# A fifth stored form set for a Strassen-like graph product, with six of a set's additions done by accumulating DMAs

## The chip, the cores and the metric

The kernel runs on one core of a Trainium2 chip. The metric is the device time of one execution in microseconds (us), as the median of several runs.

The engines are named as in the profile. PE is TensorE and does the matrix products, PEld is its weight load, DVE is VectorE, ACT is ScalarE, POOL is GpSimd and SP is SyncE. SP only issues DMAs here. SP's and POOL's queues are worked off in order.

## The reference, cut to what matters

Four graph layers run one after the other on `x` (8 batches, 2048 nodes, 64 features). Each adds its result to `x` and normalises over the features. All of them multiply by the same 2048x2048 matrix `adj`.

```
layer 0:  As = [I, A, 2*A@A - I];  out = sum_k (As[k] @ x) @ w[node, k] + b[node]
layer 1:  z = relu((A @ x) @ W0);  out = relu((A @ z) @ W1)
layer 2:  out = x @ W_self + (A @ x) @ W_neighbor + bias
layer 3:  x1 = A @ x;  x2 = 2*A @ x1 - x;  out = cat(x, x1, x2, x1, x2) @ W + bias
each:     x = layernorm(x + out)
```

Layers 0, 1 and 3 need two products with `A`, layer 2 needs one. There are seven products of a 2048x2048 by a 2048x512 matrix, all in float32.

## The kernel before

**Products.** Product 1 (the slices, up to line 1433) also writes sums of blocks of `A` to DRAM (`comb`, seven quarter matrices of four blocks plus four sums each). Products 2 to 7 are the six calls of `product` at lines 1547, 1589, 1620, 1621, 1628 and 1629. Each is one level of Strassen-Winograd on quarters: seven blocks A11, S1, A12, S2, S4, S3, A22 in this order (lines 756 to 835), where S1 to S4 are sums and differences of quarters. Each block multiplies a 1024x1024 quarter by a 1024x256 one. S3 is the difference A11 - A21, the "third difference of quarters".

**Two ways to do a block.** `inner` (line 514) does a second Strassen-Winograd level: seven products of 512x512 blocks, each from 1 MB loaded from the input or from `comb`. Its four sums of `x` (`less`, line 532) are on DVE. `fast_inner` (line 380) does a scheme with 26 products of 256x256 blocks in 13 pairs. Its sums of `x` are twelve POOL additions (lines 404 to 416), its joins are on DVE, and the matrices that it multiplies by, the 26 *forms* of a quarter, are read from DRAM (`formed`). Products 5 and 7 write their result with nodes on partitions (`onto_slot=1`). Their instructions are 128 columns wide, so those of L558 and L437 take the place of L565 and L443 in products 2, 3, 4 and 6.

**Forms.** `make_forms` (line 262) loads the four 1 MB blocks of a quarter, stores four raw parts of them as forms (`RAW`) and works through `SUMS`: 28 additions per set, ten of them on POOL (`POOLED`) and 18 on DVE, 22 of whose results are forms and six only intermediate. Each result tile is one of nine buffers `t` (`TB`). SP stores each form (256 KB) after the next addition has been written down. The next set's loads begin when the present set is nearly through (`k > SPENT`). Forms exist for four quarters (`FORMED`: S1, A12, S2, S4). S1's are made in product 2, the others at the start of product 3. Products 3 to 7 use all four. S3, A11 and A22 always go through `inner`.

**Order of work.** Results of a block go to the "pump", a queue of feature jobs (`hand_over`, line 682). In product 2 the pump is held. Four `feature0` jobs run after S2 (line 804), and the remaining twelve at the start of product 3 (line 713). A `feature0` job is eight steps of twelve PE instructions (L1519), followed by work on DVE (L1529), on ACT (L1533) and on POOL (L1539, L1542). The ACT results `s` have two buffers. `Pump.run` hands out steps of side jobs, `make_forms` first and `prepare_sums` (four DVE sums for the next `inner`, line 698) after it, at a rate per step: 1.28 after S2, 1.08 at the start of product 3. A step in which a postponed normalisation does something gives one side step less. Side steps that are left at the end are written down behind the last job.

**Order on an engine.** What passes through `tc.keep_in_program_order` stays where the program has it. Other instructions may be moved by the scheduler. `inner`'s `less` is pinned like this while the pump is held (line 530), so in all of product 2 after S1.

**After S3.** `last` (line 815) adds v and u, in products 5 and 7 also adds the result into its place in `xy`, and hands the job over. With `inner` it runs block by block as S3 proceeds; with `fast_inner` `last_all` does all four blocks behind S3's last join.

Of the kernel before, what the change touches and what calls it, by code (L numbers as in the profile page):

```python
# [9 lines left out]
F32 = mybir.dt.float32  # L10
AF = mybir.ActivationFunctionType
ALU = mybir.AluOpType
# [4 lines left out]
P = 128  # L17
# [4 lines left out]

A11, A12, A22, S1, S2, S3, S4 = range(7)
A21 = 7
FORMED = (S1, A12, S2, S4)

# [8 lines left out]
ROWS = ((0, 0), (1, 0), (0, 1), (1, 1))  # L37
RAW = {11: (2, 2), 14: (1, 1), 19: (0, 2), 23: (1, 0)}
SUMS = (
    (16, (0, 1), (0, 3), 1), (5, (2, 0), (2, 3), 1), ("d", (2, 1), (2, 2), 1), ("c", (0, 0), (0, 2), 1),  # L40
    (6, 16, (1, 3), 0), (18, 6, "d", 1), (21, (1, 1), "d", 1), (4, 21, (1, 2), 1),
    (1, (1, 3), (2, 3), 1), (2, 1, (2, 0), 1), (15, 2, "c", -1), (0, "c", (1, 0), 0),
    (20, (1, 2), 0, -1), (10, (3, 1), (3, 2), 1), ("f", 10, (3, 3), 1), (17, "f", 1, -1),
    (7, (0, 1), 10, -1), ("b", (0, 0), (1, 0), 1), (12, (0, 3), (1, 3), 1), (24, (3, 0), (3, 2), 1),
    (3, (2, 0), 24, -1), ("a", (1, 1), (2, 1), 1), (8, (3, 0), (2, 0), -1), (22, (3, 1), (0, 1), -1),
    (9, 7, "b", -1), ("e", 24, (3, 3), 1), (13, "e", 12, -1), (25, 3, "a", -1),
)
HALF = {13: 0, 22: 0, 8: 1, 17: 1}
POOLED = {5, 18, 4, 15, 20, 17, 12, 22, 9, 25}
SPENT = 24  # L50


def unit(i, j):
# [89 lines left out]
def kernel(  # L143
# [28 lines left out]
    RING = 4  # L172
    TB = 9
    LANDING = 4
    BLK = TG * GW

    big = ctx.enter_context(tc.tile_pool(name="big", bufs=1))
# [59 lines left out]
    pieces = []  # L237
    p_mm = p_y = None

    def load(q, s, forms=False):  # L240
        nonlocal loads
        loads += 1
        turn = loads % (RING + 3)
        pool = ring2 if ring2 is not None and turn >= RING else ring
        a = pool.tile([P, TG, TG, P], F32, tag="a", name="a")
        flat = a.rearrange("p n m c -> p (n m c)")
        if forms:
            size = min(4, len(SLOT) - 4 * s) * GW
            fetched = nc.sync.dma_start(flat[:, :size], formed[q][s][:, :size])
        elif q in (A11, A12, A22) and s < 4:  # L250
            i, j = {A11: (0, 0), A12: (0, 2), A22: (2, 2)}[q]
            fetched = nc.sync.dma_start(a, blocks[i + s // 2, j + s % 2])
        else:
            fetched = nc.sync.dma_start(flat, comb[q][s])
        if ring2 is not None and loads <= RING + 3:

            tc.keep_in_program_order(fetched)
        if pieces and loads > RING and loads % 3 == 0:
            tc.keep_in_program_order(pieces.pop(0)())
        return a  # L260

    def make_forms(*qs):
# [1 line left out]

        pin = tc.keep_in_program_order

        def store(q, n, f):
            k = SLOT[n]
            dst = formed[q][k // 4][:, ts(k % 4, GW)]
            nc.sync.dma_start(dst.rearrange("p (n m c) -> p n m c", n=2, m=2), f)  # L270

        coming = [load(qs[0], s) for s in range(4)]
        for _ in range(LANDING):
            yield
        for i, q in enumerate(qs):
            tiles, coming, made, done = coming, [], {}, []

            def raw(i, k):
                a, b = ROWS[i]
                return tiles[2 * a + k // 2][:, 2 * b : 2 * b + 2, 2 * (k % 2) : 2 * (k % 2) + 2, :]  # L280

            def source(f):
                return raw(*f) if isinstance(f, tuple) else made[f]

            for n, ik in RAW.items():
                store(q, n, raw(*ik))
            for k, (n, a, b, sign) in enumerate(SUMS):
                f = sums.tile([P, 2, 2, P], F32, tag="t", name="form", bufs=TB)
                if sign == 0:
                    pin(nc.vector.scalar_tensor_tensor(f, source(a), -1.0, source(b), ALU.mult, ALU.subtract))  # L290
                else:
                    eng = nc.gpsimd if n in POOLED else nc.vector
                    pin(eng.tensor_tensor(f, source(a), source(b), ALU.add if sign > 0 else ALU.subtract))
                made[n] = f
                if not isinstance(n, str):
                    done.append((q, n, f))
                yield
                while len(done) > 1:
                    store(*done.pop(0))
                if k > SPENT and len(coming) < 2 and i + 1 < len(qs):  # L300
                    coming.append(load(qs[i + 1], len(coming)))
            for job in done:
                store(*job)
            while len(coming) < 4 and i + 1 < len(qs):
                coming.append(load(qs[i + 1], len(coming)))

    def product(src, feature, between=None, rate=1, own=None, pin=False, runs=None, onto_slot=None, ends=False, fast=(), forms={}):

# [401 lines left out]
            return [make_forms(*forms[q]), prepare_sums(b)] if q in forms else []  # L710

        if waits:
            pump.run(None, side(A11, b11), 1.08)
            pump.hold = False
        pump.pass_mark()

# [84 lines left out]
            fast_inner(S2, t2, InTile(u), None, join_all)  # L801
        else:
            inner(S2, t2, *onto(u, u, then=join))
        pump.run(runs.get(S2, 0), side(S2, b22), 1.28)
        if S4 not in fast:
            inner(S4, b22, *onto(c, c, (0, 1)), ready=ready)
        elif give:
# [153 lines left out]
    if True:  # L961
# [490 lines left out]
        if True:  # L1452
# [91 lines left out]


            RUNS = {A12: 1, S2: NP}
            product(1, then(feature0, 0, gap=4), lambda: pump.add(sum_wn()), rate=4, runs=RUNS, forms={S2: (S1,)})


    late = p_z = None  # L1550
# [35 lines left out]
        nc.vector.scalar_tensor_tensor(part(g, p, 0), z, 0.0, part(g, p, 0), ALU.max, ALU.add)  # L1586
        yield

    product(0, feature1a, to_late, pin=True, fast=FORMED, forms={A11: (A12, S2, S4)})
    def both_terms(src, w, b):  # L1590

        def own(g, p):
# [86 lines left out]
```

## Time and profile before

| what | value |
|---|---|
| median of three runs | 1648.97 us (1647.35 to 1649.34) |
| the profiled execution: its own time | 1647.88 us |
| the profiled execution: its span | 1646.0 us |
| PE busy in the span | 1623.3 us, 99% |
| PEld, DVE, POOL, ACT busy | 1154.6, 1122.0, 574.5, 308.7 us |
| PE clock granted, mean | 0.998 |
| DMA | 429.47 MB, 261 GB/s |

The profiled execution's time has 1.9 us around its span and is 1.1 us below the median. A matrix product in float32 shows as two PE instructions, which overlap: the mean duration of one (say 592 ns) is longer than the distance to the next (429 ns). What a block costs is read from the chain of waits, where rows give a start, a length and a count. Stages in us from the span's start: product 1 to 209, product 2's blocks to 306 and from 389 to 464, `feature0` from 306 to 389 and from 464 to 711, products 3 to 7 from 715 on.

### The profile page before, as it was taken

The page shows a single profiled execution, that of the slowest core. Times are in us where ns is not written, and L with a number is a line of the kernel's source. Part 1 is how long each engine was busy: PE and PEld are TensorE (multiplying, and loading weights), DVE is VectorE, ACT ScalarE, POOL GpSimd, SP SyncE. Part 2 cuts the span into 40 slices and gives each one's busy share as a digit, 9 for nine tenths or more (in the row PEclk, how much of TensorE's full clock was granted, in tenths as well). Part 3 has the DMA queues.
Part 4 walks back from the last instruction along what each step waited for, and adds up shares of the span by engine and source line. Part 5 has one row for each costly group of instructions (what it writes and reads, how often), then busy time and mean ns, then how long its engine had stood idle before and what let it go on. Part 6 is the DMA issues. An engine that isn't in the chain of part 4 may idle for free.

```text
span 1646.0 us, 23252 instructions
## 1 busy us (share of the span) xinstructions
PE 1623.3 (99%) x8886; PEld 1154.6 (70%) x8886; DVE 1122.0 (68%) x1889; ACT 308.7 (19%) x870; POOL 574.5 (35%) x582
## 2 busy tenths in 40 slices
PE   9999999999999999999999999999999999999998
PEld 5998944444444444438865787589999788669998
DVE  5996885686458878846753477974688556644687
ACT  0210100143024444421111111221111112100111
POOL 1121100284037778764502350034512441025510
PEclk9999999999999999999999999999999999999999
DMA  8999999746853645278777776566888866677885
GB/s 315 358 389 370 334 342 326 250 141 237 307 178 123 203 141 187 101 310 312 277 287 262 288 280 253 208 227 234 295 293 301 292 234 213 237 255 282 310 307 175
DMA packets 101390, 429.47 MB, mean 261 GB/s; under 512 B 10752, under 2 KB 31616, under 8 KB 61856
## 3 DMA queue, kind: packets, MB, share of 16 engines
q1 hardware_dynamic: 87616, 380.34, 64.8%
q0 software_dynamic: 12016, 46.27, 7.5%
q8 instruction: 71, 1.16, 0.3%
q10 hardware_dynamic: 1648, 1.38, 0.3%
q14 instruction: 39, 0.32, 0.1%
HBM read 346.16 MB, written 81.79 MB: 260 GB/s over the span
## 4 chain that ended last, share of the span: by engine, by line
PE 94%; DVE 3%; DMA 1%; issue 1%; POOL 0%; ACT 0%; ACTq 0%; SPq 0%; DVEq 0%; POOLq 0%
PE y L1519 19%; PE mm L443 15%; PE mm L437 10%; PE mmb L565 10%; PE mmc L565 7%; PE mma L565 7%; PE ps_n L1301 6%; PE mmb L558 4%; PE ps_i L1215 3%; PE z L1573 3%; PE mmc L558 2%; PE mma L558 2%; PE z L1602 2%; PE ps_n L1255 1%; PE pt L1564 1%
## 5 line engine op out<-in xcount | busy, mean ns | idle before, releaser
L1539 POOL TENSOR_TENSOR s<-s 128x512 f32<-128x512 f32 (+2 forms) x192 | 166.2, 865 | 254.3 <-ACT s L1533 244.1
L1529 DVE SCALAR_TENSOR_TENSOR xy<-y,e_sb,xy 128x128 f32<-128x128 f32 x512 | 179.4, 350 | 65.3 <-PE y L1519 49.4
L1533 ACT ACTIVATE s<-y,e_sb 128x128 f32<-128x128 f32 x512 | 139.3, 383 | 196.2 <-PE y L1519 178.3
L565 PE MATMUL mmb<-a,t 128*128 128x512 f32 x360 | 161.9, 592 | 0.0
L443 PE MATMUL mm<-a,f 128*128 128x256 f32 x576 | 135.1, 380 | 1.1 <-POOL f L389 1.0
L1519 PE MATMUL y<-wn,xT 64*128 64x512 f32 x512 | 131.4, 590 | 0.0
L1519 PE MATMUL y<-wn,C 64*128 64x512 f32 x512 | 131.2, 589 | 0.0
L1519 PE MATMUL y<-wn,tT 64*128 64x512 f32 x512 | 131.1, 589 | 0.0
L389 POOL TENSOR_TENSOR f<-T 128x512 f32<-128x512 f32 x20 | 26.5, 1340 | 276.7 <-PE mmb L565 124.7
L565 PEld LDWEIGHTS mmb<-a,t 128*128 128x128 f32 x360 | 67.3, 190 | 79.4 <-issue 78.7
L443 PEld LDWEIGHTS mm<-a,f 128*128 128x128 f32 x576 | 108.7, 190 | 17.7 <-POOL f L389 1.9
L437 PE MATMUL mm<-f,a 128*128 128x128 f32 x768 | 92.4, 275 | 0.0
L1519 PEld LDWEIGHTS y<-wn,xT 64*128 64x128 f32 x512 | 49.5, 187 | 60.9 <-issue 57.3
L1519 PEld LDWEIGHTS y<-wn,tT 64*128 64x128 f32 x512 | 49.6, 187 | 60.2 <-issue 59.7
L1519 PEld LDWEIGHTS y<-wn,C 64*128 64x128 f32 x512 | 49.5, 187 | 60.4 <-issue 60.4
L437 PEld LDWEIGHTS mm<-f,a 128*128 128x128 f32 x768 | 89.0, 192 | 0.1
L476 DVE TENSOR_TENSOR p<-p,mm 128x512 f32<-128x512 f32 x60 | 41.0, 684 | 61.3 <-PE mm L443 41.7
L319 DVE TENSOR_TENSOR u<-mmb,p 128x512 f32<-128x512 f32 x44 | 30.2, 686 | 67.5 <-PE mmb L565 58.1
L466 DVE TENSOR_TENSOR C<-C,mm 128x512 f32<-128x512 f32 x80 | 54.2, 684 | 29.3 <-PE mm L443 22.3
L565 PE MATMUL mma<-a,T 128*128 128x512 f32 x160 | 72.1, 593 | 0.0
L1023 POOL DMA_DIRECT2D comb<-si x29 | 22.0, 758 | 137.8 <-DVE si L1014 137.8
L558 PE MATMUL mmb<-t,a 128*128 128x128 f32 x576 | 67.3, 275 | 0.0
(243 smaller groups left out, 3024.7 us busy)
## 6 DMA issues: line engine op xcount, KB each, us to landing
a<-comb SPq DMA_DIRECT2D x127, 1024.0 KB, 5.0
a<-form SPq DMA_DIRECT2D x120, 1024.0 KB, 4.8
a<-in_blocks SPq DMA_DIRECT2D x43, 1024.0 KB, 4.9
comb<-si POOLq DMA_DIRECT2D x29, 1024.0 KB, 10.6
form<-form SPq DMA_DIRECT2D x88, 256.0 KB, 2.8
a<-in_slices SPq DMA_DIRECT2D x15, 1024.0 KB, 10.9
comb<-so POOLq DMA_DIRECT2D x15, 1024.0 KB, 12.8
a<-form SPq DMA_DIRECT2D x20, 512.0 KB, 4.8
```

The costliest lines, as they stand in the source:

```text
L437: nc.tensor.matmul(ps[:, ts(2 * h + j, P)], a[:, j, m, :], x[:, m, :], start=(start and h == j == m == 0), stop=(m == 1), skip_group_check ...
L443: nc.tensor.matmul(ps[:, ts(h, GW // 2)], x[:, m, :], a[:, :, m, :], start=(start and h == m == 0), stop=(m == 1), skip_group_check=True,)
L466: nc.vector.tensor_tensor(out, out, view(v), op)
L558: nc.tensor.matmul(to, a[:, k, m, :], xb[:, m, :], start=(start and opens and m == 0), stop=(m == TG - 1), skip_group_check=True,)
L565: nc.tensor.matmul(ps, xb[:, m, :], a[:, :, m, :], start=(start and m == 0), stop=(m == TG - 1), skip_group_check=True,)
L1215: nc.tensor.matmul(ps, x[:, m // 2, m % 2], s[n](m), start=(start and m == 0), stop=(m == TG - 1), skip_group_check=True,)
L1301: nc.tensor.matmul(ps[:, ts(p, GW // 2)], b(k, p), a(k // TG, k % TG), start=(start and p == k == 0), stop=(k == NT // 2 - 1), skip_group_ ...
L1519: mm = nc.tensor.matmul(y[:, b, :], terms[n][half, ts(k, P)], wn[half, n, h * DH : (h + 1) * DH, :], start=(n == 0), stop=(n == 2),)
L1529: tc.keep_in_program_order(nc.vector.scalar_tensor_tensor(acc, y[:, :, ts(d, F)], e, acc, ALU.mult, ALU.add))
L1533: nc.scalar.activation(s[:, d], y[:, :, ts(d, F)], AF.Copy, scale=e)
L1539: nc.gpsimd.tensor_tensor(s[:, :n], s[:, :n], s[:, n : 2 * n], ALU.add)
L1573: nc.tensor.matmul(z[:, k, :], aT[:, ts(k, P)], wd[:, w, :], start=(n == 0), stop=(n == len(terms) - 1),)
```

## The change

S3 becomes a fifth formed quarter. Its set is made after S2 in product 2, in the place of S1's, whose set moves to the start of product 3 as the first of four. S3 goes through `fast_inner` in products 2 to 7.

Six of the 28 additions of a set (forms 5, 4, 15, 18, 9, 25; sign 2) are not done on an engine any more. SP stores the first operand in the form's place in DRAM, and some steps later POOL issues a DMA that adds the second operand onto that place. A set has 22 engine additions left, seven of them on POOL and 15 on DVE. The order of `SUMS` is another one. Loads of the next set start at `k >= 12`. When several sets are made, each set's last two blocks land in buffers `T` and not in the ring. The rates become 1.1 and 1.16.

```
-FORMED = (S1, A12, S2, S4)
+FORMED = (S1, A12, S2, S4, S3)
 SUMS = (
+    (5, (2, 0), (2, 3), 2), ("c", (0, 0), (0, 2), 0), (16, (0, 1), (0, 3), 1), ("d", (2, 1), (2, 2), 1),
+    (0, "c", (1, 0), -1), (21, (1, 1), "d", 1), (4, 21, (1, 2), 2), (1, (1, 3), (2, 3), 1),
+    (2, 1, (2, 0), 1), (15, "c", 2, 2), (6, 16, (1, 3), 0), (18, "d", 6, 2), (20, (1, 2), 0, -1),
+    (10, (3, 1), (3, 2), 1), ("f", 10, (3, 3), 1), (17, "f", 1, -1), (7, (0, 1), 10, -1),
+    ("b", (0, 0), (1, 0), 0), (9, 7, "b", 2), (24, (3, 0), (3, 2), 1), (3, (2, 0), 24, -1),
+    ("a", (1, 1), (2, 1), 0), (25, 3, "a", 2), (8, (3, 0), (2, 0), -1), (22, (3, 1), (0, 1), -1),
+    (12, (0, 3), (1, 3), 1), ("e", 24, (3, 3), 1), (13, "e", 12, -1),
 )
-POOLED = {5, 18, 4, 15, 20, 17, 12, 22, 9, 25}
-SPENT = 24
+POOLED = {20, 17, 22, 12, 8, 13, 1}
+AHEAD_OF_NEXT = (12, 12, 12, 27)
...
+    JOIN = 2
...
+        def fetch(q, s):
+            return load(q, s, home=None if len(qs) == 1 or s < 2 else sums.tile(
+                [P, NT // 2, 4 * F], F32, tag="T", name="T", bufs=3
+            ).rearrange("p t c -> p (t c)").rearrange("p (n m c) -> p n m c", n=TG, m=TG))
...
+            def settle(step):
+                while done and done[0][0] < step:
+                    _, n, f = done.pop(0)
+                    nc.sync.dma_start(slot(q, n), f)
+                while joins and joins[0][0] + JOIN < step:
+                    _, n, f = joins.pop(0)
+                    pin(nc.gpsimd.dma_start(slot(q, n), f, accum_op=ALU.add))
...
             for k, (n, a, b, sign) in enumerate(SUMS):
+                if sign == 2:
+                    done.append((step, n, source(a)))
+                    joins.append((step, n, source(b)))
+                    continue
...
                 yield
-                while len(done) > 1:
-                    store(*done.pop(0))
-                if k > SPENT and len(coming) < 2 and i + 1 < len(qs):
-                    coming.append(load(qs[i + 1], len(coming)))
-            for job in done:
-                store(*job)
-            while len(coming) < 4 and i + 1 < len(qs):
-                coming.append(load(qs[i + 1], len(coming)))
+                settle(step)
+                while i + 1 < len(qs) and len(coming) < 4 and k >= AHEAD_OF_NEXT[len(coming)]:
+                    coming.append(fetch(qs[i + 1], len(coming)))
+            settle(step + JOIN + 2)
...
-            pump.run(None, side(A11, b11), 1.08)
+            pump.run(None, side(A11, b11), 1.16)
...
-        pump.run(runs.get(S2, 0), side(S2, b22), 1.28)
+        pump.run(runs.get(S2, 0), side(S2, b22), 1.1)
...
-            product(1, then(feature0, 0, gap=4), lambda: pump.add(sum_wn()), rate=4, runs=RUNS, forms={S2: (S1,)})
+            product(1, then(feature0, 0, gap=4), lambda: pump.add(sum_wn()), rate=4, runs=RUNS, forms={S2: (S3,)}, fast=(S3,))
...
-    product(0, feature1a, to_late, pin=True, fast=FORMED, forms={A11: (A12, S2, S4)})
+    product(0, feature1a, to_late, pin=True, fast=FORMED, forms={A11: (S1, A12, S2, S4)})
```

## The prediction

> **What bounds the kernel now.** I read the page first: shares, then the chain that ended last, then the same chain in order of time, then the waits of PE, then the queues around the one place where PE stands still.
>
> ```profile
> span 1646.0 us, 23252 instructions
> ...
> PE 1623.3 (99%) x8886; PEld 1154.6 (70%) x8886; DVE 1122.0 (68%) x1889; ACT 308.7 (19%) x870; POOL 574.5 (35%) x582
> ...
> PE 94%; DVE 3%; DMA 1%; issue 1%; POOL 0%; ACT 0%; ACTq 0%; SPq 0%; DVEq 0%; POOLq 0%
> ```
>
> PE is busy 99% of the span, at full clock, and it is the chain. A change gains by what it takes from PE's work or from the 23 us in which PE stands, and loses by what it makes PE wait for.
>
> The chain in order of time gives a block its price: 216 instructions of plain `fast_inner`; an `inner` with 128 columns, whose seven products take 3.57 each; a plain `inner` from 1268.31 to 1292.34, where the next block begins; and three `fast_inner` with 128 columns in one piece (624).
>
> ```profile
> 918.75 46.62 PE mm L443 x216
> ...
> 1218.28 3.57 PE mma L558 x32
> ...
> 1268.31 3.44 PE mma L565 x8
> ...
> 1292.34 24.17 PE mm L443 x112
> ...
> 1494.34 69.69 PE mm L437 x624
> ```
>
> The longest wait of PE is at product 3's first load (waits: us, times, longest), which stands behind the forms' stores in SP's queue (start, length, count) and delays PE's first product:
>
> ```profile
> PE mma L565 <- DMA a<-in_blocks: 3.6, 1, 3.6
> ```
>
> ```profile
> 674.79 33.40 SPq L270 DMA_DIRECT2D form<-form  x11
> 708.25 0.42 SPq L252 DMA_DIRECT2D a<-in_blocks  x1
> ```
>
> ```profile
> 715.03 5.29 PE L565 MATMUL mma<-a,xy 128*128 128x512 f32 x8 [3.61 <-DMA a<-in_blocks]
> ```
>
> **Term 1, S3 by 26 products: -9.9 us.** Plain `inner`: 1292.34 - 1268.31 = 24.03. Plain `fast_inner` has 104 instructions: 46.62 / 216 x 104 = 22.45. It saves 1.58, in products 2, 3, 4 and 6: 6.3. With 128 columns `inner` takes 7 x 3.574 = 25.02 and `fast_inner` 208 x 69.69 / 624 = 23.23, so 1.79, in products 5 and 7: 3.6. All of it is on PE's path. Loads fall too (6.5 MB for 7 MB a block). Nothing of PE's work is added: the forms are made on DVE, POOL and DMA.
>
> **Term 2, the start of product 3: -3.8 (0 to -5.5).** SP's last form store waits for POOL's last form (706.58 to 707.84), the loads stand behind it, and the first lands at 715.0, 6.7 after its issue. PE was through at 711.4. It stands 3.6, then runs its first product in 5.29 instead of 3.44, so 5.5 in all. Counting the pump's steps by the rates (96 job steps, 12 of them with a normalisation): before, 1.08 x 96 - 12 = 91 side steps are handed out of the 4 + 84 + 4 wanted, and the last form goes out at job step 91. After, 1.16 x 96 - 12 = 99 for 4 + 88 + 4, and the last form goes out at step 88. Three job steps of 12 x 0.215 = 2.6 us are 7.7 us: the loads go out near 700.6, and land before 711.4. Two ring buffers are free for them, since a set's last two blocks land elsewhere. What is late next: the loads that use the freed space of `feature0` go out after POOL's last addition (718.38). With the 5.0 of such a load they land at 723.4, and the fourth product wants one at 711.4 + 3 x 3.43 = 721.7. That gives 1.7 back.
>
> **Term 3, S3 to A22 in product 2: +2.3 (0 to +3.7).** There `less` is pinned behind all earlier DVE work. Before, DVE needs only two additions and two sums until PE's second product:
>
> ```profile
> 440.02 0.69 DVE L319 TENSOR_TENSOR C<-mmc,C 128x512 f32<-128x512 f32 x1 [2.02 <-PE mmc L565]
> 440.75 0.69 DVE L319 TENSOR_TENSOR C<-C 128x512 f32<-128x512 f32 x1
> 441.36 0.68 DVE L534 TENSOR_TENSOR t<-T 128x512 f32<-128x512 f32 x1
> 442.07 0.69 DVE L534 TENSOR_TENSOR t<-T,t 128x512 f32<-128x512 f32 x1
> ```
>
> ```profile
> 443.25 3.60 PE L565 MATMUL mmb<-a,t 128*128 128x512 f32 x8
> ```
>
> After, behind S3's last product stand the last joins (0.69 + 0.75), four additions of `last_all` (2.9) and two sums (1.4): 5.7. A22's first product covers 3.43. Its third and fourth sum, if they came first, would add 1.4. If the sums were moved ahead it costs nothing.
>
> **Term 4, the same place in the others: +2.4 (0 to +8).** There the sums are not pinned, and the trace shows A22's already during S4 (an L534 at 1210.28, S3 starts at 1218.28). In products 3, 4 and 6 this costs nothing. In 5 and 7 `last_all` is eight additions: 1.4 + 8 x 0.7 = 7.0 after S3's end, before it was 3.1 (S3's end 1614.14, last addition through at 1617.2). So DVE, busy without a gap from 1614 to 1631, runs 4.0 later. Its `u` after A22's second product began at 1621.5 and must be done by 1624.87, 2.8 to spare. 4.0 - 2.8 = 1.2, twice.
>
> **Term 5, waits inside the new fast blocks: +1.7.** In the 20 fast blocks of before PE waits 3.3 (for DVE, L437), 1.5 (for DVE, L443) and 1.0 (for POOL): 0.29 a block, times six. The twelve POOL additions of a block (257.4 / 20 = 12.9 us) lie beside S4's 22.45 and more.
>
> **Term 6, making five sets: +1.0 (0 to +11).** One set beside 82 us of `feature0` as before; four sets instead of three beside 247 us.
>
> ```profile
> 464.00:580.00 116.00, 116.00 (x543) 52.41 (x544) 89.81 (x215) 50.11 (x180) 81.32 (x97) 1.00 0.46 150
> 580.00:708.00 128.00, 128.00 (x600) 57.85 (x598) 103.22 (x244) 57.13 (x204) 102.83 (x118) 1.00 0.42 140
> ```
>
> PE (second number) is busy all the time, DVE (fourth) 193, POOL (sixth) 184, DMA under half. So the additions saved are worth nothing by themselves, and what is added must fit. DVE: 4 x 15 = 60 additions for 3 x 18 = 54, +5 us, 198 of 244. POOL: 48 groups of `s` at 3.1 (199.9 / 64) are 150; forms 28 x 1.43 = 40 for 30 x 1.43 = 43; new are 24 accumulating DMAs.
>
> ```profile
> L1023 POOL DMA_DIRECT2D comb<-si x29 | 22.0, 758 | 137.8 <-DVE si L1014 137.8
> ...
> form<-form SPq DMA_DIRECT2D x88, 256.0 KB, 2.8
> ...
> form<-a SPq DMA_DIRECT2D x16, 256.0 KB, 5.4
> ```
>
> No accumulating DMA is in the trace. The nearest rows are POOL's other issues, 0.55 (128 KB) to 0.76. At 0.76 they are 18, and POOL stands at 208 of 247. Each must also wait, on POOL, until the first operand's store has landed; behind it stand the `s` additions, behind those ACT, PSUM and PE. The store goes out two side steps (2 x 2.6 us) earlier and lands in 2.8, for a raw block in 5.4, at the most in 8.0. So five of six find it landed. The first of a set, behind four raw stores, may wait up to 2.8, four times 11 us in all; `s` has two buffers, and ACT waits 17.9 us for POOL today without PE showing it. I take 1.0, near the row that is hidden.
>
> A page of the Trainium skill speaks against these DMAs: "DMA: Bandwidth & Descriptors", "Two DMAs through the same engine are not ordered", says that the engine which issues a dependent DMA has to wait for the first one's semaphore, the same queue being no substitute. By "Anatomy of one DMA — SWDGE (gpsimd) path" a 256 KB transfer would take, as an estimate, 2.0 + 0.6 us, and an issue right behind its store would hold POOL for so long. "Collectives: The Full Stack", "The bandwidth ceiling: the fold count and why AG ≠ RS ≠ AR", says that a DMA which adds reads two sources and runs at half the rate. No run here shows that yet; with DMA at 0.46 or less it would leave the sum as it is.
>
> **The sum.** -9.9 - 3.8 + 2.3 + 2.4 + 1.7 + 1.0 = -6.3. Against the profiled execution's own time: 1647.88 - 6.3 = 1641.6. The median lies 1.1 higher: 1648.97 - 6.3 = 1642.7. About 0.2%, 3.3 us, is what a measurement of this kernel can tell from no change. With every open term at its good end it is -9.9 - 5.5 = -15.4, 1633.6.
>
> **Rivals.**
>
> Product 3's start keeps its wait (0.16). POOL ends its forms later because of the DMAs, or another load is late. Term 2 is then 0, the sum -2.5: 1646.5, no change. For it: POOL's tail sets both the last store and the freed space. Against: 7.7 us of lead.
>
> POOL becomes the bound (0.14), **slower**. If a DMA holds POOL for the store's landing each time, it costs 0.76 + 2.8 = 3.56, 24 of them 85, and POOL needs 150 + 40 + 85 = 275 in 247 us: +28, about 1670. It decides from (247 - 190) / 24 = 2.4 us a DMA, and the gain is gone at 2.6. For it: a kind of DMA without a row, and POOL transfers that land after 10.6 us in product 1. Against: issue rows of 0.76, and the two steps between.
>
> A22's sums are moved ahead nowhere (0.06), slower. Products 2, 3, 4, 6 lose 2.3 each, 5 and 7 1.4 + 5.6 + 1.4 - 3.57 = 4.9 each, 19.0 for terms 3 and 4: -9.9 - 3.8 + 19.0 + 1.7 + 1.0 = +8.0, 1657. Against it stands the L534 at 1210.28.
>
> The change doesn't do what it says (0.02): S3's forms are not ready in product 2, and PE waits before S3. The last addition onto DRAM goes out at side step 24 of 34, and S4 with 24 us lies between. It would take a landing of over 40 us; 10.6 to 12.8 are POOL's rows. At some 12 us lost: 1655.
>
> **How the numbers follow.** Forecast 0.62, its own range 1634 to 1646. Faster 0.62; same 0.16; slower 0.14 + 0.06 + 0.02 = 0.22. The range takes in the no-change case, 1655 and 1657, and leaves out POOL as the bound: 1634 to 1658.
>
> **What would show it.** Right: PE's total falls by about 10 us; S3 is L443 or L437 in six products; no wait of PE for `in_blocks` near 711; a PE gap of about 2 us after A22's first product in product 2; POOL's accumulating issues near 0.76 with PE at 116 of 116 in the `feature0` stage. Wrong: PE gaps among L1519 with POOL without idle time, or accumulating issues that last over 2.4 us.

## The result and the profile after

The changed kernel takes 1665.21 us (median of four runs, 1663.51 to 1667.63), the kernel before 1648.99 beside it. The ratio is 1.0101, interval 1.0084 to 1.0119: 16.2 us slower, where the forecast was 1642.7 and the range ended at 1658. The page after has these lines in place of the three shown of before:

```profile
span 1661.7 us, 23828 instructions
...
PE 1624.5 (98%) x9046; PEld 1204.0 (72%) x9046; DVE 1150.8 (69%) x1916; ACT 313.7 (19%) x882; POOL 676.2 (41%) x673
...
PE 82%; DVE 10%; POOL 3%; DMA 2%; issue 2%; ACT 1%; SPq 0%; DVEq 0%; POOLq 0%; ACTq 0%
```

S3 takes less of PE's work, yet PE is no less busy (the same work ran slower, as is seen below), and PE's share of the chain falls from 94% to 82%. DVE (10% for 3%), POOL (3% for none) and DMA (2% for 1%) have more of it now. The waits of PE (us, times, longest) name who was late. Lines behind the new code are numbered some 18 higher than before (L565 is now L583, L1519 is L1537, L1533 is L1551, L1539 is L1557), and differ by a few more in the experiments. The profile of run 1 below was taken at a lower granted clock (0.943), so no block's length is read from it. The waits, with a line of before first:

```profile
PE mma L565 <- ACT p L577: 2.2, 1, 2.2
```

```profile
PE mma L583 <- ACT p L595: 6.2, 1, 6.2
PE mma L583 <- ACT s L1551: 4.7, 1, 4.7
...
PE y L1537 <- DVE xy L1547: 3.0, 3, 2.5
PE y L1537 <- ACT s L1551: 2.8, 1, 2.8
...
PE mmb L583 <- issue: 2.3, 1, 2.3
PE mmb L576 <- DVE u L337: 2.1, 1, 2.1
```

The wait for `in_blocks` is gone, as forecast. Five others have come, and one of 2.2 has become 6.2. PE's matmuls, in order of time, give each block's length, from its first product to the next block's first (us; PE's idle time inside, up to and with the next block's start, in brackets where it changed):

| block | before | after | difference |
|---|---|---|---|
| product 2, S2 and four `feature0` jobs | 106.73 | 107.28 | +0.55 |
| product 2, S4 (idle before its third product) | 26.63 (2.23) | 33.37 (6.24) | +6.74 |
| product 2, S3 | 24.03 | 22.45 | -1.58 |
| product 2, A22 and twelve jobs, to product 3 | 275.21 (3.61) | 288.48 (12.38) | +13.27 |
| product 3, A11 | 25.73 | 26.95 | +1.22 |
| products 3, 4 and 6, S3 and A22 | 190.60 | 184.71 | -5.89 |
| product 5, S3 and A22 | 50.02 | 52.35 (2.08) | +2.33 |
| product 7, S3 and A22 | 56.98 | 55.74 | -1.24 |

These sum to +15.4, and 0.4 more was lost before product 2's S2, of 15.8 in the span. So the saving is there, and two places of product 2 lose 20 us. The trace shows three accidents of queue order in them.

**A. x sums on POOL ahead of `feature0`'s last sums.** POOL's timeline (start, length, operation) at the start of S4:

```profile
388.25 2.50 POOL L407 TENSOR_TENSOR f<-T 128x512 f32<-128x512 f32 x2
...
393.54 1.29 POOL L410 TENSOR_TENSOR f<-d,T 128x512 f32<-128x512 f32 x1
394.79 3.46 POOL L1557 TENSOR_TENSOR s<-s 128x512 f32<-128x512 f32 x3
```

Six additions of S3's new `fast_inner`, which nobody needs for nearly 30 us more, stand ahead of the last `s`. Behind those wait a square and a copy on ACT (L899, L595) and PE, until 403.48.

**B. An accumulation ahead of its store, on POOL.** The chain in order of time, where one set begins:

```profile
601.63 14.31 DMA T<-comb
616.01 5.39 DMA form<-T
621.41 6.12 DMA form<-form
...
630.56 1.23 POOL s L1557
...
634.97 2.17 ACT s L1551 x8
637.18 7.14 PE y L1537 x24
```

The late load is not one of the set that POOL is at. It is the next set's. The program has that set's raw stores (L302) behind the whole present set; the scheduler put them ahead in SP's queue. The load of 601.63 lands 14.3 us later, the next set's raw stores wait for it, and the present set's stores (L296) stand behind them:

```profile
616.98 0.49 SPq L302 DMA_DIRECT2D form<-T  x1
...
618.11 12.80 SPq L296 DMA_DIRECT2D form<-form  x9
```

Among these is the first operand of form 4. It goes out at 621.41 and lands at 627.5, and the DMA that adds to it waits for that on POOL. The set's first accumulating DMA (`form<-a`, form 5) did not wait:

```profile
612.60 1.22 POOL L299 DMA_DIRECT2D form<-a  x1
...
628.06 1.20 POOL L299 DMA_DIRECT2D form<-T  x1 [5.80 <-DMA form<-form]
```

Three such waits make 8.0 us (5.80, 1.96 and 0.23). What is queued behind the DMA on POOL holds up ACT, and ACT PE (2.79).

**C. A square root on ACT ahead of `feature0`'s last scaling.** ACT's timeline at product 3's start, before and after:

```profile
711.55 2.18 ACT L1533 ACTIVATE s<-y,e_sb 128x128 f32<-128x128 f32 x8 [2.97 <-PE y L1519]
714.20 0.21 ACT L897 ACTIVATE rs<-rs 128x16 f32<-128x16 f32 x1 [0.47 <-DVE rs L894]
```

```profile
732.08 0.21 ACT L915 ACTIVATE rs<-rs 128x16 f32<-128x16 f32 x1 [5.17 <-DVE rs L912]
732.20 2.16 ACT L1551 ACTIVATE s<-y,e_sb 128x128 f32<-128x128 f32 x8
```

The two have changed places. The square root waits 5.17 for DVE, the scaling behind it holds the PSUM bank that product 3's first matmul needs:

```profile
734.41 6.51 PE L583 MATMUL mma<-a,xy 128*128 128x512 f32 x8 [4.65 <-ACT s L1551]
```

### The profile page after: what moved, and what is told of

The parts are those of the page before. It is cut to its first block, busy times and chain, and to the rows that moved or that the text cites. A ratio compares the mean times of both kernels' runs of the same rounds, so it can differ in the third digit from the quotient of the medians.

```text
span 1661.7 us, 23828 instructions
## 1 busy us (share of the span) xinstructions
PE 1624.5 (98%) x9046; PEld 1204.0 (72%) x9046; DVE 1150.8 (69%) x1916; ACT 313.7 (19%) x882; POOL 676.2 (41%) x673
## 3 DMA queue, kind: packets, MB, share of 16 engines
q10 hardware_dynamic: 1648, 1.38, 0.3%
## 4 chain that ended last, share of the span: by engine, by line
PE 82%; DVE 10%; POOL 3%; DMA 2%; issue 2%; ACT 1%; SPq 0%; DVEq 0%; POOLq 0%; ACTq 0%
PE mm L461 20%; PE mm L455 13%; PE y L1537 10%; PE mmb L583 7%; PE ps_n L1319 6%; PE mma L583 5%; PE mmc L583 5%; PE ps_i L1233 3%; DVE xy L1547 3%; PE z L1591 2%; PE z L1620 2%; PE ps_n L1273 2%; PE mmb L576 2%; POOL s L1557 2%; DMA T<-comb 1%
## 5 line engine op out<-in xcount | busy, mean ns | idle before, releaser
L1557 POOL TENSOR_TENSOR s<-s 128x512 f32<-128x512 f32 (+2 forms) x192 | 184.4, 961 | 213.9 <-ACT s L1551 203.5
L461 PE MATMUL mm<-a,f 128*128 128x256 f32 x768 | 180.1, 379 | 1.1 <-POOL f L407 1.0
L1551 ACT ACTIVATE s<-y,e_sb 128x128 f32<-128x128 f32 x512 | 139.0, 386 | 197.9 <-PE y L1537 173.9
L461 PEld LDWEIGHTS mm<-a,f 128*128 128x128 f32 x768 | 144.7, 190 | 22.8 <-POOL f L407 1.9
L1537 PE MATMUL y<-wn,xT 64*128 64x512 f32 x512 | 134.7, 595 | 5.7 <-DVE xy L1547 3.0
L1537 PE MATMUL y<-wn,tT 64*128 64x512 f32 x512 | 134.6, 595 | 0.0
L1537 PE MATMUL y<-wn,C 64*128 64x512 f32 x512 | 134.5, 594 | 0.0
L583 PE MATMUL mmb<-a,t 128*128 128x512 f32 x264 | 119.2, 593 | 2.3 <-issue 2.3
L455 PE MATMUL mm<-f,a 128*128 128x128 f32 x960 | 115.5, 275 | 0.0
L455 PEld LDWEIGHTS mm<-f,a 128*128 128x128 f32 x960 | 111.2, 192 | 0.1
L484 DVE TENSOR_TENSOR C<-C,mm 128x512 f32<-128x512 f32 x110 | 74.8, 684 | 44.4 <-PE mm L461 35.2
L1537 PEld LDWEIGHTS y<-wn,xT 64*128 64x128 f32 x512 | 53.3, 188 | 65.1 <-issue 55.5
L1537 PEld LDWEIGHTS y<-wn,C 64*128 64x128 f32 x512 | 54.2, 189 | 57.0 <-issue 57.0
L1537 PEld LDWEIGHTS y<-wn,tT 64*128 64x128 f32 x512 | 54.0, 188 | 56.7 <-issue 56.5
L583 PEld LDWEIGHTS mmb<-a,t 128*128 128x128 f32 x264 | 49.4, 190 | 61.6 <-issue 61.0
L461 PE MATMUL mm<-a,T 128*128 128x256 f32 x320 | 77.0, 380 | 0.0
L461 PEld LDWEIGHTS mm<-a,T 128*128 128x128 f32 x320 | 59.6, 190 | 7.9
L899 ACT ACTIVATE sq<-xy 128x1024 f32<-128x1024 f32 (+3 forms) x35 | 34.4, 984 | 156.2 <-DVE xy L481 52.0
```

Of the source, the lines that this page charges most:

```text
L455: nc.tensor.matmul(ps[:, ts(2 * h + j, P)], a[:, j, m, :], x[:, m, :], start=(start and h == j == m == 0), stop=(m == 1), skip_group_check ...
L461: nc.tensor.matmul(ps[:, ts(h, GW // 2)], x[:, m, :], a[:, :, m, :], start=(start and h == m == 0), stop=(m == 1), skip_group_check=True,)
L484: nc.vector.tensor_tensor(out, out, view(v), op)
L583: nc.tensor.matmul(ps, xb[:, m, :], a[:, :, m, :], start=(start and m == 0), stop=(m == TG - 1), skip_group_check=True,)
L1537: mm = nc.tensor.matmul(y[:, b, :], terms[n][half, ts(k, P)], wn[half, n, h * DH : (h + 1) * DH, :], start=(n == 0), stop=(n == 2),)
L1551: nc.scalar.activation(s[:, d], y[:, :, ts(d, F)], AF.Copy, scale=e)
```

## The experiments

Ratios are to the kernel before, run on the same chip. Edits are against the changed kernel unless it says otherwise.

**1. Later accumulations.** `JOIN = 2` becomes `JOIN = 5`.

> Changed kernel with JOIN = 5 instead of 2: every accumulating DMA is issued three additions later, nothing else moves. Theory A (in the stage of feature0, POOL waits for the store of an accumulation's first operand to land, 8.0 us in three waits, 5.80 of them at 622.3 to 628.1 us, and TensorE stalls 2.46 and 2.79 us right behind them): the three waits shrink below 2 us together, the two stalls go, and the stage from product 2's S4 to product 3's start becomes 7 to 10 us shorter than in the changed kernel (ratio to the kernel before 1.004 to 1.006). Rival B (POOL is late by the work it issues, forms and accumulations of about 1 us each, wherever they stand): the waits on the store shrink, but the stage stays within 3 us (ratio 1.008 to 1.012). Neither theory lets the boundary from S2 to S4 in product 2 move by more than 2 us.

1.0055 (1.0038 to 1.0072). Its profile shows no wait of POOL for a store at all, one stall of 1.37 us in place of 2.46 and 2.79, and ACT's scaling (4.4 us) still at product 3's start. By the time theory A holds: issuing the accumulations later is worth some 7 us. Not all of it is accident B, since PE's idle time at S4 fell too, from 6.24 to 3.82, which neither theory expected.

**2. x sums in program order.**

```
+            held = tc.keep_in_program_order if pump.hold else lambda inst: inst
-                nc.gpsimd.tensor_tensor(out, a, c, ALU.subtract)
+                held(nc.gpsimd.tensor_tensor(out, a, c, ALU.subtract))
```

and the same for the additions.

> Changed kernel, with POOL's additions and subtractions of the third-difference product (its x sums) kept in program order in product 2, so that the six of them that stood ahead of feature0's last sums on POOL (388 to 395 us) come behind these. Theory A (those six, 6.4 us of POOL, delay the sum, square and product that the first matmuls of S4 wait for): TensorE's idle time at the start of S4 in product 2 falls from 6.24 us to under 3, S4 takes 26 to 28 us instead of 33.4, and the kernel becomes 5 to 7 us faster than the changed one (ratio to the kernel before 1.006 to 1.007). Rival B (the accumulations and waits of the form making have put POOL that late already): S4 stays at 32 us or more and the ratio at 1.009 to 1.011. A third way: the x sums come so late that S3 starts late, and the gain of S4 stands as a wait at the start of S3.

1.0059 (1.0036 to 1.0081). S4 takes 28.23 with 2.20 idle for 6.24: accident A is shown. But the block from A22 to product 3 grows from 288.48 to 292.77, its first stall from 2.46 to 5.02.

**3 and 4. The two halves of the change apart.** Each is the kernel before with one of them:

```
3: five sets, S3 by forms, all 28 additions on DVE and POOL
-FORMED = (S1, A12, S2, S4)
+FORMED = (S1, A12, S2, S4, S3)
-            pump.run(None, side(A11, b11), 1.08)
+            pump.run(None, side(A11, b11), 1.38)
4: the changed make_forms, with four sets and S3 by inner
```

> Kernel before with the fifth form set (S3, in product 2 and later) alone: all 28 additions of a set stay on the engines as they were, no accumulating DMA, the loads as before; five sets are made in place of four, with the feeding of side work at product 3's start raised to 1.38 for the four sets made there. Theory A (the DMAs and the waits they bring cost more than the additions they replace): faster than the changed kernel by 3 to 8 us, ratio to the kernel before 1.001 to 1.006, with product 3's start still waiting for its forms by 3 us or more. Rival B (the accumulations are what makes a fifth set affordable): slower than the changed kernel by 5 us or more, ratio 1.013 to 1.02, with VectorE and POOL stalls in the stage of feature0 larger than the 12.4 us of TensorE idle time of the changed kernel.

> Changed kernel's way of making forms (six accumulating DMAs a set, the early loads, the new order of additions) with the four sets of the kernel before; the set of S1 is made in product 2, S3 is done by the ordinary way in every product. Theory A (the way of making is itself a loss in the stage of feature0, by POOL's waits, and the fifth set gives back about 8 us): 5 to 10 us of loss in that stage against the kernel before, product 3's start gains 3 us, ratio 1.001 to 1.005, and the boundary from S2 to S4 in product 2 is as before (26.6 us for S4), since no x sums of S3 stand there. Rival B (the way of making gains, the fifth set is what costs): ratio 0.996 to 0.999.

The fifth set alone: 1.0058 (1.0043 to 1.0073), with 7.7 us of waiting for product 3's loads and 5.50 at S4. The accumulations alone: 1.0048 (1.0033 to 1.0062), with S4 28.22, the A22 block 282.50 for 275.21, and product 3's start waiting 4.56 for ACT's scaling in place of its loads. So each half loses 8 to 10 us by itself, theory A in both. In 4 the idle time at S4 is 2.22, as before; the block is 1.6 longer because the granted clock fell behind that pause (see the last section). 4 also differs from before in more than the DMAs: the order of the additions, the earlier loads, their place in `T` and the rates come with them. It looks as if the DMAs were worse than additions. But 4.0 of the 7 us by which 3 is faster than the changed kernel lie in A22 of product 5 (25.13 for 29.12), which is taken up under term 4 below, and run 11 reverses the order.

**5. Cures 1 and 2 together.**

> Both cures together: JOIN = 5 and the x sums of the third-difference product pinned on POOL in product 2. Theory A (two independent causes, each worth what it gave alone: 6 us of the ratio 1.0101 to 1.0055 by the later accumulations and 5 to 6 us by the pinned sums): S4 in product 2 at 28 us or less, no wait of POOL for a store in the stage of feature0 over 1 us, ratio to the kernel before 1.000 to 1.003. Rival B (the pinned sums move POOL's lateness into the stage of feature0, where its first stall grew from 2.46 to 5.02 us when they were pinned alone): S4 at 28 us but the stage of feature0 as long as in the changed kernel, ratio 1.004 to 1.007. In both, TensorE still waits 4 us or more at product 3's start for ScalarE's last scaling, and 2.3 us after A22's first product in product 2.

1.0036 (1.0023 to 1.0050), between the two theories. S4 takes 26.68, POOL waits once for a store (2.34), the A22 block still takes 286.52, and PE waits 5.08 at product 3.

**6. Norms later.** `gap=4` becomes `gap=5` in product 2, on top of 5.

> The kernel of the later accumulations and pinned sums, with the gap of feature0's norms in product 2 raised from 4 to 5 half tiles, so that ScalarE's last square root stands behind feature0's last scaling instead of ahead of it. Theory A (the wait at product 3's start, 4.65 us in the changed kernel, is ScalarE's square root waiting for VectorE with the scaling that frees the PSUM bank queued behind it): that wait becomes 1.5 to 3 us (the scaling's own 2.2 us remain), the slow first product shrinks, and the kernel is 2 to 4 us faster than the one without the gap. Rival B (the forms or the next sums are late too): the wait changes its name, at the same length, and the time moves by less than 1 us.

1.0155 (1.0136 to 1.0174), 20 us slower than 5. The square root did go behind, but all norms moved, product 3's wait became one of 5.80 for loads, and S1 waits 8.52 for an x sum of POOL. It says nothing on accident C: the edit was too wide.

**7 and 8. What the accumulation itself costs.** 7: `accum_op=ALU.add` left out. 8: the DMA left out.

> Changed kernel, with the six accumulating DMAs of each set made plain copies: same size, place, queue and waits, and six of a set's 28 additions are left out of the computation. Theory A (what costs is the issue on POOL and the wait for the first store, not the adding): issue on POOL within 0.1 us of the changed kernel's 0.87 to 1.21 us, the waits for stores stay at 6 to 10 us in all, time within 3 us of the changed kernel. Rival B (the adding itself slows the DMA engines, as a transfer that reads two sources, and with them the stores and loads): landing under 4 us instead of 5.4 to 6.5 us, waits under 5 us, 4 to 8 us faster.

> Changed kernel without its accumulating DMAs: the first operand of each of the six sums is stored and nothing is added to it, so six of a set's 28 additions are left out of the computation. It gives the most that a cheaper accumulation could give back. Theory A (accumulations cost POOL about 1 us each and three waits of 8 us in all, and these are what stalls the stage of feature0): the stage from A22 in product 2 to product 3's start falls from 288.5 to 276 to 281 us, with no stall over 1 us but the one after A22's first product (2.27 us) and the one at product 3's start; the kernel is 7 to 12 us faster than the changed one. Rival B (the engines' additions and the early loads are late anyway): the stage stays above 284 us. The boundary from S2 to S4 in product 2 stays above 31 us if it is the x sums' order alone, and falls towards 28 if the accumulations ahead of it had a part.

7 took 1654.9 (span 1653.1), 8 took 1650.7 (span 1648.9), one run each. POOL's groups (busy, mean ns of one) and DMA rows (count, KB, us to landing), first with adding (after), then without (7):

```profile
L299 POOL DMA_DIRECT2D form<-form x20 | 17.6, 944 | 0.5 <-DMA form<-form 0.2 <-issue 0.2
...
form<-form POOLq DMA_DIRECT2D x20, 256.0 KB, 5.9
```

```profile
L299 POOL DMA_DIRECT2D form<-form x20 | 11.2, 562 | 0.6 <-DMA form<-form 0.5
...
form<-form POOLq DMA_DIRECT2D x20, 256.0 KB, 3.0
```

Adding doubles the landing and takes 0.38 us more of POOL per issue, which is rival B's side; POOL's waits for stores are 5.6 in all for 8.0. Of 7's gain of 8.6 in the span 4.0 lies in product 5, which is taken up under term 4 below. The other 4.6 would be the cost of the adding, but executions of the changed kernel alone differ by 4.1. In 8 the A22 block falls to 279.89, with one stall of 0.76 besides the waits after A22's first product and at product 3, as theory A has it. S4 falls to 30.32 for 33.37, so the accumulations ahead of it had a part in its loss. Yet its span is still 3.0 above before. Going by this execution, even accumulations that cost nothing would not have made this order pay: 4.21 at S4, 2.27 after A22's first product, 4.51 at product 3 and 2.07 in product 5 remain.

**9, 10 and 11. The square root, A22's sums, and the same without DMAs.** 9 is 5 with

```
+        norm.pin = tc.keep_in_program_order if pump.hold else norm.pin
         norm.root()
+        norm.pin = lambda inst: inst
```

10 is 9 with `pump.hold` replaced by `(pump.hold and q != A22)` in `inner`'s pin. 11 is 3 with the cures that apply to it, and the rate 1.6.

> The kernel of the later accumulations and pinned x sums, with the gap of 4 kept and the square root of feature0's norms kept in program order in product 2, which puts ScalarE's last square root behind feature0's last scaling (in the changed kernel it stands ahead of it) and leaves the rest of ScalarE's order as it is. Theory A (the wait of 5.08 us at product 3's start is that square root's wait for VectorE): the wait becomes 2 to 3 us, which is the scaling's own 2.2 us and the bank, and the kernel is 2 to 4 us faster than the one with the two cures, ratio to the kernel before 1.001 to 1.003. Rival B (the blocks of product 3 or its sums come as late): a wait of 4 us or more under another name, time within 1 us.

> As the kernel with the square root behind, and the four sums of A22 in product 2 no longer kept in program order on VectorE, so that they stand ahead of S3's last additions. Theory A (term 3 of the prediction, measured 2.27 us of TensorE's waiting after A22's first product and 1.9 us of a slower product behind it): the wait goes, 2.3 to 4 us faster than the kernel with the square root behind, ratio to the kernel before 0.998 to 1.001. Rival B (feature0's jobs behind it run at the pace of VectorE and POOL, so that what TensorE gains there it waits for later): the wait goes, and the time from A22 to product 3's start shrinks by less than 1 us.

> Kernel before with the fifth set, all 28 additions on the engines, and three of the cures: pinned x sums, square root behind, free sums of A22; the feeding of side work at product 3's start raised to 1.6 so that the forms end, and product 3's first loads start, earlier. Theory A (the accumulating DMAs are a loss against additions on the engines, as 1658.0 us against 1665.2 in the uncured kernels shows): S4 in product 2 at 28 us or less, the wait for product 3's first loads under 5 us in place of 7.7, and a ratio to the kernel before of 0.994 to 0.999, at least 2 us below the kernel with accumulations and the same cures. Rival B (with the cures in, VectorE and POOL are the limit of the stage of feature0, where the six additions a set count): as slow as the kernel with accumulations and the same cures, or slower, with stalls of TensorE behind VectorE's scaling there.

9 gives 0.9984 (0.9975 to 0.9994): faster than before, and 9 us faster than 5, more than expected. ACT and PE at product 3's start in 9:

```profile
717.29 2.17 ACT L1555 ACTIVATE s<-y,e_sb 128x128 f32<-128x128 f32 x8 [2.98 <-POOL s L1561]
719.88 0.22 ACT L917 ACTIVATE rs<-rs 128x16 f32<-128x16 f32 x1 [0.42 <-DVE rs L914]
```

```profile
719.51 3.70 PE L585 MATMUL mma<-a,xy 128*128 128x512 f32 x8 [2.35 <-ACT s L1555]
```

The wait is 2.35 and the first product takes 3.70 for 6.51. The same line also mended S4, where the same square root stood ahead of the same scaling: 24.48 for 26.68.

10 gives 0.9966 (0.9951 to 0.9980), an interval that overlaps 9's; its median is 3.0 us below 9's. The wait after A22's first product is gone. In the profile the A22 block is only 0.6 shorter, and a stall of 2.12 has come at 642.47, behind a wait of POOL for a store of 4.92. By these blocks it is rival B: what PE gains there, it waits for later. But the profiled execution is the slowest of 10's five (1645.1, the others 1641.5 to 1643.4), and by the median it is theory A. Which of the two holds stays open.

11 gives 1.0057 (1.0042 to 1.0072), 14 us slower than 10. Theory A falls. Stalls of 1.82, 4.19, 4.86 and 2.64 stand in the `feature0` stage; PE waits there four times, 13.5 us in all, for DVE's scaling, as rival B has it. So with the orders mended the changed way of making forms is the better one. That the DMAs are the reason is likely, as DVE is what PE waits for and they take additions off it, but not shown: 10 and 11 also differ in the order of the additions, the early loads and the rate, and between 1.38 and 1.6 no rate was run.

**12, 13 and 14. What is still open.** 12 is the kernel before with 9's lines alone. 14 is the changed kernel with 9's lines alone. 13 is 10 with

```
+                    if q != A22 or s != 5 or tail is not None:
                         pump.step(pump.rate)
```

> Kernel before with one line of the cures alone: the square root of feature0's norms kept in program order in product 2. It tells how much of the cured kernel's gain belongs to the change and how much the kernel before could have had without it. Theory A (the square root's place was good in the kernel before at product 3's start, where the last scaling ended 1.3 us before the loads came, and bad at the start of S4, where TensorE waits 2.23 us for a square, a copy and a product behind it): S4's wait falls under 0.5 us, product 3's wait for its loads stays at 3 to 4 us, 2 to 3 us faster, ratio 0.998 to 0.999. Rival B (the place of the square root changes nothing here): ratio 0.9995 to 1.0005. Under theory A the cured kernel, 0.9966, owes about a third of its gain to this line; under B all of it is the change's.

> The kernel with the square root behind and A22's sums free in product 2, and one step of side work less after A22's second product of matmuls in products 5, which puts the partial sum that TensorE waits for (2.07 us, and a product of 5.46 us behind it in place of 3.4 to 3.6) ahead of the second norm on VectorE instead of behind it. Theory A (term 4 of the prediction, which put 1.2 us on product 5: the price is 4 us there because the wait is followed by a slow product): A22 in product 5 takes 25.0 to 25.2 us in place of 29.1, the kernel is 3 to 4.5 us faster, ratio to the kernel before 0.993 to 0.995. Rival B (the norm that comes later holds up another matmul or product 6): A22 is shorter and product 6's first two parts are longer, time within 1 us.

> Changed kernel with one line of the cures alone: the square root of feature0's norms kept in program order in product 2; the accumulations wait 2 steps and the x sums are free, as in the changed kernel. Theory A (this square root, ahead of a scaling on ScalarE, is the costliest of the changed kernel's accidents, 9 us where the other two are cured): product 3's wait falls from 4.65 to 2.4 us and its A11 from 26.95 to 24.2 us, S4's stays above 3 us, the two stalls behind POOL's waits for stores stay, 5 to 9 us faster than the changed kernel, ratio to the kernel before 1.0045 to 1.007. Rival B (it only pays where POOL is on time): within 3 us of the changed kernel, ratio above 1.008.

12: 0.9990 (0.9981 to 1.0000). S4's wait went from 2.23 to 1.16 (not under 0.5), product 3's to 3.08. So some 1.5 us of the cured kernels' gain, if it is real, needed no change of the forms.

14: 1.0078 (1.0061 to 1.0096), some 4 us faster than the changed kernel with intervals that overlap, between the theories. The wait at product 3 is 2.35, A11 24.14. S4's wait stays at 6.25, the two stalls at 2.46 and 2.59. The square root is worth some 4 us there and 9 in run 9, where POOL is on time.

13: 0.9956 (0.9944 to 0.9969), 1641.26 us, the fastest. A22 in product 5 takes 26.02 for 29.11, its wait 0.61 for 2.07, product 6's first part is 0.12 longer. In that block it is theory A, at three quarters of its price; as a ratio the step from 10 is 0.0010, some 1.6 us, with intervals that overlap. The page of 13:

```profile
span 1640.5 us, 23834 instructions
...
PE 1615.1 (98%) x9046; PEld 1199.3 (73%) x9046; DVE 1154.5 (70%) x1916; ACT 313.6 (19%) x882; POOL 678.9 (41%) x673
```

PE's work fell by 8.2 against before, and the standing time rose from 23 to 25.

## Why the prediction was wrong

By its own terms, from the table (predicted, measured in the changed kernel, and the same blocks of run 13):

| term | predicted | measured | run 13 |
|---|---|---|---|
| 1 and 5, S3 by forms with its waits | -8.2 | -11.0 | -11.0 |
| 2, start of product 3 | -3.8 | +2.3 | -2.9 |
| 3, after A22's first product | +2.3 | +2.3 | 0 |
| 4, the same in products 5 and 7 | +2.4 | +4.7 | +1.7 |
| 6, making five sets | +1.0 | +17.3 | +6.5 |
| the rest | 0 | +0.4 | +0.3 |

**Term 1** was right to 0.1 us a block (24.03 to 22.45, 25.01 to 23.23), and term 5's waits did not come.

**Term 2 failed at "what is late next".** Its mechanism was right: the loads were issued at 720.00 and were in time. But the next wait was in the trace of before, and the step did not look at it: ACT's last scaling ended at 711.55 + 2.18 = 713.73, 1.3 us before the loads at 715.03. So at the most 1.3 of the 3.6 could be had, even had ACT's order stayed. With the order mended (run 9) that is what was had: the wait is 2.35, and the first product is no longer slow, 2.9 together. The order is the scheduler's, and in the changed kernel it turned against product 3 (accident C).

**Term 3** was right in size, 2.27, but partly by luck. It priced a pause at its length, although term 2's own line shows a slow product behind a pause (5.29 for 3.44). In the changed kernel the product behind this pause is not slow (3.67). In runs 2, 5, 6, 7 and 14 the granted clock fell behind the same 2.27. Whether the term is a price of the whole stays open (run 10).

**Term 4** had the right mechanism in product 5, "Its `u` after A22's second product", and the wrong size: 4.1 there, because 2.08 of waiting was followed by a slow product, and 0.5 in product 7. The slack of 2.8 was read in product 7 and taken for both. DVE, POOL and PE of the changed kernel in product 5:

```profile
1276.38 1.23 DVE L910 TENSOR_SCALAR ss<-ss 128x16 f32<-128x16 f32 x1
1277.52 0.68 DVE L337 TENSOR_TENSOR u<-mmb,p 128x512 f32<-128x512 f32 x1
```

```profile
1276.26 1.32 POOL L407 TENSOR_TENSOR d<-T 128x512 f32<-128x512 f32 x1 [2.09 <-PE mmc L576]
```

```profile
1278.25 5.47 PE L576 MATMUL mmb<-t,a 128*128 128x128 f32 x32 [2.08 <-DVE u L337]
```

In run 7 the same L910, in the same order of DVE instructions, took 0.16, `u` was in time and the 4 us were not lost; run 3 did not lose them either. In the changed kernel L910 stands beside POOL's addition of 1276.26 and ends with it. In run 7 that addition began 1.06 behind L910, and a later small instruction (L920, 1.24 us) stands beside it. So the price hangs on which of DVE's small instructions POOL's addition meets; what sets that was not found.

**Term 6 failed twice**, and it is the step that made the forecast wrong: 17.3 for 1.0. Its 1.0 was chosen "near the row that is hidden", a mean over the stage, with 0 to 11 as its ends. In the `feature0` stage it cost 10.0 (13.27, less 2.27 of term 3 and 1.04 more at product 3), inside those ends. The working put the wait at "The first of a set, behind four raw stores", up to 2.8 by the stores' landing. The first did not wait in any of the five sets (0.04 at most). The second did, 1.96 and 5.80 in two sets, and the raw stores it stood behind were the next set's. The wait was 5.8 long because the store itself was issued late: the next set's loads landed up to 14.3 us after their issue, its raw stores stood behind these on SP, the first operand's store behind those. That ACT "waits 17.9 us for POOL today without PE showing it" was no reserve: it is a sum of six waits, the longest 3.0, and one of 5.8 goes through two `s` buffers.

The other 7.3, 6.7 of it at S4, has no step in the prediction. Term 5 counted the fast block's twelve POOL additions as lying "beside S4's 22.45", and did not ask what they might be put ahead of on POOL in a stage where POOL is in the chain.

**The rivals.** "Product 3's start keeps its wait" was right that another event is late, and put 0 on it. "POOL becomes the bound" named the right engine and the wrong way: its price was a throughput, 3.56 us for each of 24 DMAs. They cost 0.9 to 1.2 each, two of the 24 waited over 1 us, and POOL was busy for 213 of 288 us in that stage. POOL was late at single moments, not overloaded. "Moved ahead nowhere" and "doesn't do what it says" did not come about.

With the three orders mended the same work takes 1645.7, with 10's and 13's edits 1641.3. That this is close to the forecast of 1642.7 is in part luck. The stage of `feature0` still costs 8.1 more than before in run 13 (282.07 for 275.21, with 1.26 less of waiting at product 3), where term 6 had 1.0; POOL still waits 5.0 for a store there, and PE stands 0.89, 2.46 and 2.25. S4 gives 2.1 back (24.49 for 26.63), half of which run 12 had without the change, and term 3's wait is gone by 10's edit. So the saving of term 1 is shown, and what the sum missed is the queues' order and a price of making the forms that stays with these three orders mended.

## What to carry to other kernels

Where a wait is to be removed, read from the same trace when each other input of the waiting instruction was ready: the gap to the second latest is the most that can be gained. Where work is added to an in-order queue that a stage's chain passes through, price the single latest moment, not the mean: list what the scheduler may put ahead of the chain's instructions, and what an added wait needs, back through each queue to a load. And compare two ways of doing a thing only after the accidents of order are out of both: uncured, the old way of making forms won by 7 us, 4 of them by a timing in product 5; cured, the new way won by 14.

## What the runs showed of the hardware

An adding DMA of 256 KB from POOL landed in 5.9 us, the same without adding (run 7) in 3.0, and its issue held POOL for 0.94 in place of 0.56. "Collectives: The Full Stack" of the Trainium skill, "The bandwidth ceiling: the fold count and why AG ≠ RS ≠ AR", says of reduce-scatter that it runs at half the rate of all-gather, which only copies, because the add has to read two sources; the landings here, of single DMAs, agree with it in size.

A pause of PE can cost more than itself. Two stretches (their length, PE's busy time and count, the granted clock, the DMA share, GB/s): behind the pause of 4.65 at product 3 in the changed kernel, and behind that of 2.35 at the same place in run 13.

```profile
734.40:737.60 3.20, 3.19 (x4) 0.50 0.00 0
```

```profile
719.00:722.00 3.00, 3.00 (x7) 1.00 0.05 19
```

That is why the 6.24 and 4.65 us pauses cost 2.8 to 3 us more in a first product of 6.4 to 6.5 for 3.6. The length of the pause alone doesn't decide: the clock stayed at 1.00 behind a pause of 2.88 in run 2 and fell behind one of 2.07 in run 14.

What decides can be read from the clock records of before, after and runs 2 to 14. From 20 us on up to the last matmuls, the clock was at half only for stretches of 3.41, 6.83 or 10.24 us, and within a profile these start whole multiples of 3.413 us apart. In the changed kernel they start at 402.18, 569.43, 637.70, 733.27 and 1279.41, that is 49, 20, 28 and 160 times 3.413 apart. Cut each profile into windows of this grid and add up PE's pauses in each. Of the windows at full clock, all 6931 with up to 1.99 us of pauses are followed by full clock, and all 47 with 2.03 or more by half clock. So the 2.88 of run 2, which a window's edge cut into 1.65 and 1.23, cost nothing more, and the 2.07 of run 14, inside one window, did.

"TensorE: Matmul & The Clock Gate", "Part 1: The HAM clock gate (the "warmup" mystery)", puts the fall to half behind an idle window of some 3.4 us that runs freely. The 3.413 us and the fixed grid agree with it. That the whole window must be idle does not: 2.03 of the 3.41 were enough here, and the measurement decides.
